# Layers 0 and 2 of a four-layer network: the rows of maxima alone are turned, and added to the queries by VectorE

## The chip, the core and the metric

The kernel runs on one core of a Trainium2 chip. A core has a matrix engine (TensorE, PE in the profile, with its weight loads as PEld), a vector engine (VectorE, DVE), a scalar engine (ScalarE, ACT), a general engine (GpSimd, POOL) and a queue engine that issues DMAs (SyncE, SP). Each runs a list of instructions of its own; semaphores make one wait for another. Work memory is SBUF, 128 partitions wide; the matrix engine writes to PSUM, which here is handed out in banks of 512 float32 columns. The metric is the device time of one execution in microseconds (us), and of several executions the median.

## The reference

The input `x` (16 batches, 256 tokens, 256 features) goes through four layers, each an attention part and a feed-forward part, every one behind a layer norm and with a residual sum. The change touches two attentions: the first part of layer 0, and the one inside layer 2's feed-forward part. Both have 16 heads of 16 features.

```python
# layer 0: queries are the normed x, memory is ctx (keys: first 256 features, values: last 256)
Q = _split_heads(query, 16) * 16 ** (-0.5)
logits = einsum('bhqd,bhkd->bhqk', Q, Kh) + b
logits = logits + MASK_VALUE * (1.0 - valid)[:, None, None, :]
weights = softmax(logits, axis=-1)
out = einsum('bhqk,bhkd->bhqd', weights, Vh)

# layer 2, inside its feed-forward part: causal self-attention
h = _rms(x, n1_w)
q = _rms(heads(wq), qn_w); k = _rms(heads(wk), kn_w); v = heads(wv)
scores = einsum('bhqd,bhkd->bhqk', q, k) * 16 ** (-0.5)
scores = where(causal, scores, -inf)
ao = einsum('bhqk,bhkd->bhqd', softmax(scores), v) @ wo.T
```

A softmax subtracts each row's maximum before the exponential. How that subtraction is made is what the change is about.

## The kernel before, in words

A batch's 256 tokens are two halves of 128 (`t` is 0 or 1). In each half, `qpad` holds 128 tokens (partitions) by 16 heads by 32 slots: 16 features and 16 slots for extras. `heads_transposed` (L277 to L282) turns it into the form that the scores need: four transposes on TensorE (L281) of four heads each (4 x 32 = 128 rows) into one bank of the pool `ptr`, then one copy by ScalarE (`evac`, L150 or L152) into SBUF. The result is `QT`: rows are slots, with four heads `j` in four bands of 32 rows, and four groups `c` along the columns. Head `4c + j` sits in band `j`, group `c`. The keys `KT` have the same form (`kpad` in layer 0, filled by DMA from the transposed context).

Scores are made twice. `score_max` (L223) makes them with the query tokens as rows, in four banks of the pool `pmm`; VectorE reduces each bank to its negated row maxima (`put` in `maxima`, L635 and L1492). The reductions write into a free slot of `qpad` (slot 17 in layer 0, 16 in layer 2). Then `queries` (layer 0) or `heads_q` (layer 2) turns the whole `qpad` once more, now with the maxima, into `QM`. `probs` (L241) makes the scores a second time, with the keys as rows, from `QM` and `KT`; the key rows of that slot are 1, so the product has the maximum already subtracted, and ScalarE takes the exponential (L263). `weighted` (L272) multiplies by the values, `back` turns the result to tokens again (L653) and divides.

In layer 0 rows 17 to 31 of each band of the keys are all 1 (the whole tile is set to 1, then the 16 features and the bias row 16 are loaded over it), and slots 18 to 31 of the queries are 0. In layer 2 slot 16 of each head's key is 1 and the other extras are 0.

The four compute engines run under a hand-written order (`manual_schedule`): what the Python code calls first stands first in each engine's list. Two lists, one for even and one for odd steps, are walked through; each entry names a piece of work and by how many steps its batch is away. Entries of layer 0's even list that the change and the prediction bear on:

```python
(maxima, -2, 3), (queries, -2, 0, QMs), (t_stats, 0), (exps, -1, 2), (queries, -3, 0, QTs),
(maxima, -2, 2), (slots, 1), (t_norm, 0), (values, -1, 1), (exps, -1, 3), (values, -1, 2),
(queries, -3, 1, QTs), (maxima, -3, 0), (v_heads, -2), (queries, -2, 1, QMs), (values, -1, 3),
(scatter, 4, 4), (exps, -2, 0), (back, -1, 1), (maxima, -3, 1), (turned, 0), (values, -2, 0),
```

In the odd list of layer 0, `(exps, -1, 3), (queries, -2, 1, QMs), (slots, 1), (maxima, -3, 0), (values, -1, 3), (queries, -3, 1, QTs)` come in this order. In layer 2's even list, the first making of `QM` stands behind `(maxima, 1, 2)` and is followed on `ptr` by `turned` of the cross-attention (L336); in its odd list the second stands behind `values` of the cross-attention (L358, with VectorE's L366 and L367) and is followed on `ptr` by `places` (L1592). Layer 2 mixes these with the products of the experts (L1676, L1703).

Pools: `ptr` has one bank in both layers; `pmm` has six in layer 0 and four in layer 2. In layer 0 the tile `o` (three buffers) takes the divided result of `back`; GpSimd adds it to `x` (L656). At the end of layer 0 the key and value projections of layer 3 begin, with loads into buffers that layer 0 no longer uses (`kv_load`, L476).

Of the kernel before, what the change touches and what calls it, by code (L numbers as in the profile page):

```python
# [9 lines left out]
F32 = mybir.dt.float32  # L10
# [28 lines left out]
def tile_kernel(ctx: ExitStack, tc: tile.TileContext, a, out):  # L39
# [237 lines left out]
    def heads_transposed(dst, src, h0, on=None, scale=None):  # L277
# [4 lines left out]
        evac(dst, p, scale, on=on)  # L282

    def normalized(t, O, dst):
        rec = small(16, "rec16")
        V.reciprocal(rec, O[:, :, 16])
        V.tensor_tensor(dst, O[:, :, :16], rec.unsqueeze(2).to_broadcast([P, 16, 16]), ALU.mult)
# [156 lines left out]
    with ExitStack() as l01:  # L444
# [87 lines left out]
        with ExitStack() as l0:  # L532
# [5 lines left out]

            bk = c0.tile([B, S], F32, name="bk")
            dma(bk, a["L0_b"].unsqueeze(0).to_broadcast([B, S]))  # L540
# [16 lines left out]
            for i in range(4):  # L557
# [3 lines left out]
                qpads.append(q)  # L561

            kpads, vpads = [], []
            for i in range(3):
                k = c0.tile([P, 4, S], F32, name=f"kpad{i}")
                V.memset(k, 1.0)
                kpads.append(k)
                v = c0.tile([P, 2, 16, 32], F32, name=f"vpad{i}")
                G.memset(v, 1.0)
                vpads.append(v)  # L570
# [47 lines left out]
            def q_norm(b):  # L618
                mv, r = mvs.pop(b)
                qps[b] = qpads[2 * (b % 2) : 2 * (b % 2) + 2]  # L620
                for t in range(2):
                    normed(qps[b][t][:, :, :16], b, t, mv, r, split=16)
                    G.memset(qps[b][t][:, :, 17], 0.0)
                QTs[b] = at[0].tile([P, 4, S], F32, name="QT", tag="QT")
                QMs[b] = at[0].tile([P, 4, S], F32, name="QM", tag="QM")
                oTs[b] = at[0].tile([P, 4, S], F32, name="oT", tag="oT")

            def queries(b, t, to):
                heads_transposed(to[b][:, :, t * P : (t + 1) * P], qps[b][t], 0, A)

            def maxima(b, u):
                t, cp = u // 2, u % 2

                def put(j, sc):
                    V.tensor_reduce(qps[b][t][:, 8 * cp + j : 8 * cp + j + 5 : 4, 17], sc, AX.X, ALU.max, negate=True)  # L635

                score_max(cp, t, QTs[b], KTs[b], 32, put)
# [133 lines left out]
            for b, tag in zip(range(KV0), ("QM", "QM", "oT", "oT")):  # L771
                kv_load(b, big4(tag), at[0].tile([P, S], F32, name="mrb0", tag="mrb0"))
            for b in range(KV0):
# [499 lines left out]
    with ExitStack() as l2:  # L1273
# [14 lines left out]
        with ExitStack() as l2a:  # L1288
# [44 lines left out]
            for i in range(2):  # L1333
                q = ta([P, 16, 32], f"qpad2{i}")
                V.memset(q, 0.0)
                qpads.append(q)
                k = ta([P, 16, 32], f"kpad2{i}")
                V.memset(k, 0.0)
                V.memset(k[:, :, 16], 1.0)
                kpads.append(k)  # L1340
                v = ta([P, 2, 16, 32], f"vpad2{i}")
                G.memset(v, 1.0)
                vpads.append(v)
# [108 lines left out]
            def head_scale(b):  # L1452
# [3 lines left out]
                for t in range(2):  # L1456
                    for k, to in ((0, qpads[t]), (1, kpads[t])):
# [3 lines left out]
                        )  # L1461
                    G.memset(qpads[t][:, :, 16], 0.0)
                del rqs[b]

            def heads_q(b, t, to):
                heads_transposed(to[b][:, :, t * P : (t + 1) * P], qpads[t], 0, A, hw[:, 0:1])

# [19 lines left out]
            def maxima(b, u):  # L1487
                t, cp = u // 2, u % 2
                qp = qpads[t]

                def put(j, sc):
                    V.tensor_reduce(qp[:, 8 * cp + j : 8 * cp + j + 5 : 4, 16], sc, AX.X, ALU.max, negate=True)  # L1492

                score_max(cp, t, QTs[b], KTs[b], 32, put, mask, True)
# [632 lines left out]
```

## Time and profile before

| what | value |
|---|---|
| median of 10 runs (lowest to highest) | 3187.6 us (3185.09 to 3191.82) |
| the profiled execution, its own time | 3187.92 us |
| its span, from the first instruction to the last | 3186.1 us |
| mean granted clock of TensorE | 0.939 |
| layer 0's attention | about 20 to 400 us |
| layer 2's attentions and first experts | about 1680 to 2660 us |
| transposes of `qpad` (L281), both layers | 512, of 272 ns (median) each |
| ScalarE's copies into `QM` | 32 of 586 ns (layer 0), 32 of 687 ns (layer 2) |
| VectorE's reductions into `qpad` | 256 of 683 ns (layer 0); 256, median 552 ns (layer 2) |
| GpSimd's memsets of the maxima slot | 64, of 122 ns (layer 0) and 132 ns (layer 2) |

The page gives each engine's busy time and share of the span. A row of the timeline gives start, length, engine, line, operation, what it writes and reads, shapes and count; in brackets stand the idle time before it on its engine and what ended that. Rows of one line that follow each other closely are merged, with one start and one length for all. A window's row gives the busy time of each engine in a stretch, how many instructions it had, and the granted clock of TensorE. A busy share is an average; an engine with a low share can still be the one that others wait for at one place, since each list runs in order.

### The profile page before, as it was taken

How to read it: one execution, taken by the hardware profiler on the slowest of the kernel's cores; microseconds unless marked ns; L12 is line 12 of the kernel's file. 1: busy time of each engine (PE TensorE's matmuls, PEld its weight loads, DVE VectorE, ACT ScalarE, POOL GpSimd, SP SyncE). 2: the span in 40 equal slices, each digit the busy share in tenths (PEclk: the TensorE clock that was granted, in tenths of full speed). 3: DMA queues.
4: the chain of work that ended last, by engine and by line, in shares of the span. 5: the costliest groups of instructions: out<-in, count | busy, mean ns of one | idle time of the engine just before them, and what ended most of it. 6: DMA issues, size and time to landing. Idle time of an engine off the chain costs nothing. (4 is left out here: it accounts for less than half of the span.)

```text
span 3186.1 us, 57308 instructions
## 1 busy us (share of the span) xinstructions
PE 2833.7 (89%) x22567; PEld 2026.7 (64%) x22567; DVE 1478.4 (46%) x3848; ACT 1159.4 (36%) x2192; POOL 911.9 (29%) x1459
## 2 busy tenths in 40 slices
PE   7999889999989992999967889999999999759995
PEld 4655466666668851688854446777777777636663
DVE  7766621100146640222224666666666651047776
ACT  3654421121112210111112435656656664224443
POOL 2445530000046516010011333233333221044543
PEclk9999999999999986999976989999999999869996
DMA  6941232122035322466640012333333236242211
GB/s 256 347 155 48 69 103 86 60 79 80 23 125 190 124 96 103 127 202 200 191 149 29 28 51 87 106 105 116 106 100 115 93 96 216 76 135 58 62 36 53
DMA packets 249375, 357.07 MB, mean 112 GB/s; under 512 B 24107, under 2 KB 189019, under 8 KB 244868
## 3 DMA queue, kind: packets, MB, share of 16 engines
q1 hardware_dynamic: 230660, 305.75, 29.3%
q0 software_dynamic: 18432, 47.47, 4.6%
q8 instruction: 187, 3.06, 0.4%
q14 instruction: 96, 0.79, 0.1%
HBM read 236.40 MB, written 117.52 MB: 111 GB/s over the span
## 5 line engine op out<-in xcount | busy, mean ns | idle before, releaser
L263 ACT ACTIVATE big<-pmm 128x512 f32<-128x512 f32 (+1 forms) x512 | 237.4, 550 | 118.8 <-PE pmm L256 103.8
L909 PE MATMUL pmm<-xiT,w 128*128 128x512 f32 x512 | 224.6, 596 | 2.1 <-DVE xiT L145 2.0
L157 POOL TENSOR_SCALAR rsq<-mv 128x2 f32<-128x2 f32 x128 | 26.7, 209 | 695.5 <-DVE mv L175 677.1
L917 PE MATMUL pacc<-w,h 128*128 128x256 f32 x1024 | 223.6, 379 | 0.0
L917 PEld LDWEIGHTS pacc<-w,h 128*128 128x128 f32 x1024 | 194.6, 190 | 33.3 <-issue 7.7
L918 DVE COPY yo<-pacc 128x256 f32<-128x256 f32 x64 | 27.2, 425 | 403.6 <-PE pacc L917 403.6
L945 POOL DMA_INDIRECT y<-ye,idx x64 | 62.0, 968 | 481.6 <-issue 481.2
L635 DVE TENSOR_REDUCE qpad<-pmm 128x2 f32<-128x512 f32 x256 | 158.9, 685 | 60.4 <-PE pmm L234 57.7
L316 DVE TENSOR_REDUCE max<-pmm 128x2 f32<-128x512 f32 x256 | 159.2, 681 | 31.4 <-PE pmm L234 28.4
L909 PEld LDWEIGHTS pmm<-xiT,w 128*128 128x128 f32 x512 | 96.0, 191 | 120.4 <-issue 111.0
L1492 DVE TENSOR_REDUCE qpad<-pmm 128x2 f32<-128x256 f32 (+1 forms) x256 | 125.1, 552 | 75.2 <-PE pmm L234 55.0
L1676 PE MATMUL pf<-hf,fw 128*128 128x256 f32 x640 | 152.5, 381 | 0.0
L1376 POOL DMA_INDIRECT y<-yslots,idx x64 | 66.0, 1031 | 289.3 <-SPq L1259 273.1
L1676 PE MATMUL pf<-xf,fw 128*128 128x256 f32 x576 | 142.7, 384 | 0.1
L911 ACT ACTIVATE h<-pmm 128x512 f32<-128x512 f32 x128 | 76.3, 597 | 149.7 <-PE pmm L909 149.6
L1676 PEld LDWEIGHTS pf<-hf,fw 128*128 128x128 f32 x640 | 116.8, 190 | 15.6 <-issue 2.0
L272 PE MATMUL pacc<-big,vpad 128*32 128x256 f32 (+1 forms) x2048 | 124.0, 366 | 1.0 <-ACT big L263 0.7
L234 PE MATMUL pmm<-kpad,QT 32*128 32x256 f32 x1024 | 107.9, 427 | 9.0 <-ACT big L263 7.5
L1676 PEld LDWEIGHTS pf<-xf,fw 128*128 128x128 f32 x576 | 103.2, 190 | 18.6 <-issue 6.7
L281 PE MATMUL ptr<-ident,qpad 128*128 128x128 f32 x512 | 85.4, 291 | 24.0 <-DVE qpad L184 12.1
L174 DVE BATCH_NORM_STATS2 bnst<-x 128x6 f32<-128x256 f32 x256 | 104.4, 408 | 4.8 <-POOL x L656 2.0
L1237 PE MATMUL pacc<-wd,hb 128*128 128x256 f32 (+1 forms) x432 | 99.2, 379 | 0.0
(462 smaller groups left out, 6114.8 us busy)
## 6 DMA issues: line engine op xcount, KB each, us to landing
xe<-zero SPq DMA_DIRECT2D x24, 1024.0 KB
w<-in_w_dram SPq DMA_DIRECT2D x16, 1024.0 KB
wg<-in_w_gate_dram SPq DMA_DIRECT2D x36, 352.0 KB
wu<-in_w_up_dram SPq DMA_DIRECT2D x36, 352.0 KB
xslots<-zero SPq DMA_DIRECT2D x9, 1024.0 KB
wd<-in_w_down_dram SPq DMA_DIRECT2D x36, 256.0 KB
xi<-xslots SPq DMA_DIRECT2D x36, 256.0 KB
yslots<-yb SPq DMA_DIRECT2D x36, 256.0 KB
```

The costliest lines, as they stand in the source:

```text
L174: V.bn_stats(st, xs[b][:, t, :])
L234: T.matmul(sc[j][:, i, :nk], lhsT=QT[rows, c, t * P : (t + 1) * P], rhs=KT[rows, c, :nk], start=(mask is None), stop=True, skip_group_chec ...
L263: A.activation(e[:, :, q0:], sc[j], AF.Exp, bias=bias, scale=scale)
L272: T.matmul(O[32 * j : 32 * j + 32, i, q0:], lhsT=lhsT(kc, 8 * cp + 4 * i + j), rhs=pT[j][:, i, q0:], start=(kc == 0 and i == 0), stop=(kc ...
L281: T.transpose(p[:, c, :], src[:, h0 + 4 * c : h0 + 4 * c + 4, :].rearrange("p h d -> p (h d)"), ident)
L316: V.tensor_reduce(self.m[:, t, j, :], sc, AX.X, ALU.max, negate=True)
L635: V.tensor_reduce(qps[b][t][:, 8 * cp + j : 8 * cp + j + 5 : 4, 17], sc, AX.X, ALU.max, negate=True)
L909: T.matmul(p, lhsT=w1[:, c, f * P : (f + 1) * P], rhs=xiT[:, c, :], start=(c == 0), stop=(c == 1))
L917: T.matmul(p[:, :D], lhsT=hT[f][:, s * P : (s + 1) * P], rhs=w2[:, f, :], start=(f == 0), stop=(f == 7))
L1237: T.matmul(p[:, t, :], lhsT=h[:m, k, t * P : (t + 1) * P], rhs=wd[:m, k, :], start=(k == 0), stop=(k == 2))
L1492: V.tensor_reduce(qp[:, 8 * cp + j : 8 * cp + j + 5 : 4, 16], sc, AX.X, ALU.max, negate=True)
L1676: T.matmul(p[:, j * S : (j + 1) * S], lhsT=w[:, c, f * P : (f + 1) * P], rhs=x, start=(c == 0), stop=(c == len(src) - 1),)
```

## The change

The maxima get tiles of their own, `mx` (128 tokens by 4 bands by 32 slots, zero elsewhere), two per batch parity and half. The reductions write there: for band `j` and group `c` into slot `17 + c` (layer 0) or `16 + c` (layer 2). Making `QM` is now one transpose of `mx` and one addition by VectorE: for each of the four groups, `QT` plus the turned maxima. All four groups of a band so carry the maxima rows of all four groups, and the keys pick the right one: group `c` of the keys has a 1 in row `17 + c` (or `16 + c`) and 0 in the other three. In layer 0 the keys are filled from `own`, a small pattern that GpSimd makes; in layer 2 four memsets set it. The memset of the maxima slot on GpSimd and ScalarE's copy into `QM` are gone. `bk` and layer 0's mask rows for the key projections now use buffers of `o`.

```diff
--- before.py
+++ after.py
@@ -281,6 +281,19 @@
             T.transpose(p[:, c, :], src[:, h0 + 4 * c : h0 + 4 * c + 4, :].rearrange("p h d -> p (h d)"), ident)
         evac(dst, p, scale, on=on)
 
+    def maxima_rows(pool):
+
+        rows = [[pool.tile([P, 4, 32], F32, name=f"mx{k}{t}", tag=f"mx{k}{t}") for t in range(2)] for k in range(2)]
+        for m in rows[0] + rows[1]:
+            V.memset(m, 0.0)
+        return rows
+
+    def less_maxima(QM, QT, t, mx):
+
+        p, tok = ptr()[:, :P], slice(t * P, (t + 1) * P)
+        T.transpose(p, mx.rearrange("p j c -> p (j c)"), ident)
+        V.tensor_tensor(QM[:, :, tok], QT[:, :, tok], p.unsqueeze(1).to_broadcast([P, 4, P]), ALU.add)
+
     def normalized(t, O, dst):
         rec = small(16, "rec16")
         V.reciprocal(rec, O[:, :, 16])
@@ -536,7 +549,7 @@
             psums(l0, "ps0", 6, 1, 1)
             l0.enter_context(tc.manual_schedule(engines=BUSY))
 
-            bk = c0.tile([B, S], F32, name="bk")
+            bk = at[0].tile([P, D], F32, name="o", tag="o", bufs=3)[:B]
             dma(bk, a["L0_b"].unsqueeze(0).to_broadcast([B, S]))
             lens_i = c0.tile([B, 1], I32, name="lens_i")
             dma(lens_i, a["itok"])
@@ -560,10 +573,17 @@
                 V.memset(q[:, :, 16], 1.0)
                 qpads.append(q)
 
+            own = c0.tile([P, 4], F32, name="own")
+            V.memset(own, 0.0)
+            for j in range(4):
+                rows = own[32 * j : 32 * j + 32]
+                G.affine_select(rows, rows, [[-1, 4]], ALU.not_equal, 1.0, base=-17, channel_multiplier=1)
+            mx0 = maxima_rows(c0)
+
             kpads, vpads = [], []
             for i in range(3):
                 k = c0.tile([P, 4, S], F32, name=f"kpad{i}")
-                V.memset(k, 1.0)
+                V.tensor_copy(k, own.unsqueeze(2).to_broadcast([P, 4, S]))
                 kpads.append(k)
                 v = c0.tile([P, 2, 16, 32], F32, name=f"vpad{i}")
                 G.memset(v, 1.0)
@@ -620,19 +640,21 @@
                 qps[b] = qpads[2 * (b % 2) : 2 * (b % 2) + 2]
                 for t in range(2):
                     normed(qps[b][t][:, :, :16], b, t, mv, r, split=16)
-                    G.memset(qps[b][t][:, :, 17], 0.0)
                 QTs[b] = at[0].tile([P, 4, S], F32, name="QT", tag="QT")
                 QMs[b] = at[0].tile([P, 4, S], F32, name="QM", tag="QM")
                 oTs[b] = at[0].tile([P, 4, S], F32, name="oT", tag="oT")
 
             def queries(b, t, to):
-                heads_transposed(to[b][:, :, t * P : (t + 1) * P], qps[b][t], 0, A)
+                if to is QMs:
+                    less_maxima(QMs[b], QTs[b], t, mx0[b % 2][t])
+                else:
+                    heads_transposed(to[b][:, :, t * P : (t + 1) * P], qps[b][t], 0, A)
 
             def maxima(b, u):
                 t, cp = u // 2, u % 2
 
                 def put(j, sc):
-                    V.tensor_reduce(qps[b][t][:, 8 * cp + j : 8 * cp + j + 5 : 4, 17], sc, AX.X, ALU.max, negate=True)
+                    V.tensor_reduce(mx0[b % 2][t][:, j, 17 + 2 * cp : 19 + 2 * cp], sc, AX.X, ALU.max, negate=True)
 
                 score_max(cp, t, QTs[b], KTs[b], 32, put)
 
@@ -769,7 +791,7 @@
 
             wsrc = kv_weights([big4("QT") for _ in range(2)])
             for b, tag in zip(range(KV0), ("QM", "QM", "oT", "oT")):
-                kv_load(b, big4(tag), at[0].tile([P, S], F32, name="mrb0", tag="mrb0"))
+                kv_load(b, big4(tag), at[0].tile([P, D], F32, name="o", tag="o", bufs=3))
             for b in range(KV0):
                 for i in range(4):
                     kv_piece(b, i, wsrc, pmm, ring[0])
@@ -1336,7 +1358,8 @@
                 qpads.append(q)
                 k = ta([P, 16, 32], f"kpad2{i}")
                 V.memset(k, 0.0)
-                V.memset(k[:, :, 16], 1.0)
+                for c in range(4):
+                    V.memset(k[:, 4 * c : 4 * c + 4, 16 + c], 1.0)
                 kpads.append(k)
                 v = ta([P, 2, 16, 32], f"vpad2{i}")
                 G.memset(v, 1.0)
@@ -1459,11 +1482,15 @@
                             to[:, :, :16], qks[b, t][:, 16 * k : 16 * k + 16, :],
                             rqs[b][1][:, t, 16 * k : 16 * k + 16].unsqueeze(2).to_broadcast([P, 16, 16]), ALU.mult,
                         )
-                    G.memset(qpads[t][:, :, 16], 0.0)
                 del rqs[b]
 
+            mx2 = maxima_rows(ca)
+
             def heads_q(b, t, to):
-                heads_transposed(to[b][:, :, t * P : (t + 1) * P], qpads[t], 0, A, hw[:, 0:1])
+                if to is QMs:
+                    less_maxima(QMs[b], QTs[b], t, mx2[b % 2][t])
+                else:
+                    heads_transposed(to[b][:, :, t * P : (t + 1) * P], qpads[t], 0, A, hw[:, 0:1])
 
             def heads_k(b, t):
                 heads_transposed(KTs[b][:, :, t * P : (t + 1) * P], kpads[t], 0, A, hw[:, 1:2])
@@ -1486,10 +1513,10 @@
 
             def maxima(b, u):
                 t, cp = u // 2, u % 2
-                qp = qpads[t]
+                mx = mx2[b % 2][t]
 
                 def put(j, sc):
-                    V.tensor_reduce(qp[:, 8 * cp + j : 8 * cp + j + 5 : 4, 16], sc, AX.X, ALU.max, negate=True)
+                    V.tensor_reduce(mx[:, j, 16 + 2 * cp : 18 + 2 * cp], sc, AX.X, ALU.max, negate=True)
 
                 score_max(cp, t, QTs[b], KTs[b], 32, put, mask, True)
```

## The prediction

> **What bounds the kernel now.** I read the page first, then the busy time of each engine over stretches of layers 0 and 2, then the timeline at places where the turned queries with maxima (QM) are made. Durations and instants are of the one profiled execution: its span is 3186.1 us and its own time 3187.92 us, 0.3 us from the median of 3187.6, so the sum can be set against either.
>
> ```profile
> PE 2833.7 (89%) x22567; PEld 2026.7 (64%) x22567; DVE 1478.4 (46%) x3848; ACT 1159.4 (36%) x2192; POOL 911.9 (29%) x1459
> ```
>
> ```profile
> 30.00:200.00 170.00, 164.32 (x1858) 105.75 (x1856) 126.78 (x286) 97.87 (x186) 65.85 (x105) 1.00 0.82 309
> 1940.00:2620.00 680.00, 672.45 (x7693) 501.63 (x7692) 418.12 (x1194) 418.17 (x778) 214.08 (x376) 1.00 0.33 104
> ```
>
> The columns after the length are PE, PEld, DVE, ACT and POOL busy, then the granted clock. In the steady part of both layers PE is busy 97% and 99% of the time: no other engine's average sets the end. But DVE is at 75% in layer 0, and all engines run an order fixed by hand, so what counts is how far DVE stands behind PE at each QM. An even step of layer 0, first QM (token half 0), then the second:
>
> ```profile
> 62.75 0.66 PE L281 MATMUL ptr<-ident,qpad 128*128 128x128 f32 x4
> 62.84 2.49 DVE L635 TENSOR_REDUCE qpad<-pmm 128x2 f32<-128x512 f32 x4 [0.29 <-PE pmm L234]
> 63.33 1.97 PE L256 MATMUL pmm<-QM,kpad 32*128 32x256 f32 x16
> 64.18 0.72 PEld L256 LDWEIGHTS pmm<-QM,kpad 32*128 32x128 f32 x10 [0.30 <-DVE qpad L635]
> 65.24 0.66 PE L281 MATMUL ptr<-ident,qpad 128*128 128x128 f32 x4
> ```
>
> ```profile
> 72.06 0.66 PE L281 MATMUL ptr<-ident,qpad 128*128 128x128 f32 x4
> 72.21 2.49 DVE L635 TENSOR_REDUCE qpad<-pmm 128x2 f32<-128x512 f32 x4 [2.74 <-PE pmm L234]
> 72.64 1.07 PE L272 MATMUL pacc<-big,vpad 128*32 128x256 f32 x16
> 72.75 0.59 ACT L150 COPY QM<-ptr 128x512 f32<-128x512 f32 x1 [0.79 <-PE ptr L281]
> 73.64 1.15 PE L256 MATMUL pmm<-QM,kpad 32*128 32x256 f32 x16
> ```
>
> The reader is to see that at both places DVE is in the middle of four reductions of the *next* maxima (2.49 us) while ACT, which had been idle, empties the transposes at once, and PE goes on.
>
> **The change, part by part.** *Removed from PE:* each of 64 QM makings (2 layers, 16 batches, 2 halves) has 1 transpose instead of 4. The row says 0.66 us for four, but the next matmul starts 0.58 us after the first (62.75 to 63.33), so a transpose takes 0.145 us of PE's time, three take 0.435 us, and 64 times that is 27.8 us. This is the ceiling of the gain. The built order shows the transposes at the same places with the rest of PE's list unchanged, so the change does what it says.
>
> *Where the 0.435 us is kept.* At 91.70 (odd step of layer 0):
>
> ```profile
> 91.70 0.66 PE L281 MATMUL ptr<-ident,qpad 128*128 128x128 f32 x4
> 91.85 2.06 ACT L263 ACTIVATE big<-pmm 128x512 f32<-128x512 f32 x4 [0.53 <-PE pmm L256]
> 92.29 1.82 PE L234 MATMUL pmm<-kpad,QT 32*128 32x256 f32 x16
> 92.99 0.72 PEld L234 LDWEIGHTS pmm<-kpad,QT 32*128 32x128 f32 x10 [0.20 <-ACT big L263]
> ```
>
> The 16 scores after it take 1.82 us instead of the 1.15 us that sixteen take at 73.64, because their banks come free only with ACT's exponentials. PE arriving 0.435 us earlier would wait 0.435 us longer there. So I count the odd steps of layer 0 at nothing (bounds: 15 calls by -0.435 = -6.5 us, and 0). If the exponentials did not cover it, PE would gain that time. In layer 2 I count the saving at nothing as well, where the next scores wait for ACT or DVE (bound -0.435 for some 10 calls, -4.4 us).
>
> *Removed from ACT:* 32 copies of 0.586 us and 32 of 0.687 us; ACT idles just before most of them. *Removed from POOL:* 64 memsets of 0.12 to 0.13 us that nothing in the steady part waits for. Both at nothing: what hides them is PE, and a loss is excluded, since nothing is put in their place there.
>
> *Added to DVE:* 64 additions of 512 columns with one operand in PSUM. The nearest rows are the 128x512 tensor-tensor instructions at L510 and L1228, 0.691 and 0.687 us: I take 0.69 (the 128x512 tensor-tensor at L1404 takes the same), 44 us in all, on an engine that is not full. The price is in the queue: the addition is built directly behind the reductions that stand before it in the hand-written order, and PE's next use waits for it. The ptr pool has one bank.
>
> Layer 0, even step, first QM: the reductions end at 65.33, the addition at 66.02, and with 0.1 us to PE the next user of ptr (transposes of the new queries, 65.24 in the row) starts at 66.12: 0.88 us late. That PE saves 0.435 us in front doesn't help: the middle of its scores waits for the same reductions (64.18 row). Second QM: the reductions end at 74.70, the addition 75.39, PE's exponent scores, which read this QM, start at 75.49 instead of 73.64: 1.85 us late. Behind them stand the back transposes, ACT's exponentials and the next maxima, all shifted with PE. The same pair of rows comes back in seven even steps from 62 to 345 us: 7 x 2.73 = 19.1 us. In odd steps the addition ends before PE's next user, but for one step with routing work on DVE (0.2 us late at 135.5 us).
>
> Layer 2, even and odd step:
>
> ```profile
> 2257.91 2.49 DVE L1492 TENSOR_REDUCE qpad<-pmm 128x2 f32<-128x512 f32 x4 [1.02 <-PE pmm L234]
> 2260.04 0.28 PE L336 MATMUL ptr<-ident_bf,nmp 128*128 128x128 bf16 x2
> ```
>
> ```profile
> 2211.73 1.76 DVE L366 RECIPROCAL rT<-pacc 128x256 f32<-128x256 f32 x1 [0.79 <-PE pacc L358]
> 2213.43 0.29 PE L1592 MATMUL ptr<-ohx,before 128*128 128x16 f32 x2
> 2213.52 0.42 DVE L367 TENSOR_TENSOR uT<-pacc,rT 128x256 f32<-128x256 f32 x1
> ```
>
> Even: reductions to 2260.40, addition and hand-over to 2261.19, while L336 needs the bank at 2260.04: 1.15 us, five times. Odd: the values' reciprocal and product stand ahead, to 2213.94; with the addition 2214.73, against L1592 at 2213.43: 1.30 us, six times; the first QM of odd steps adds 0.2 us five times (2202.60 against 2202.40). Together 5.8 + 7.8 + 1.0 = 14.6 us.
>
> *Ramps.* The same reading of the first calls gives 2.5 and 1.7 us of lateness in layer 0 (at 30 and 36 us) and 8.7 us over the first seven late calls of layer 2 (1740 to 1911), where PE has idle time to give: bounds 0 and 12.9, I take 3 + 5, and 1 for the last call of layer 2.
>
> *Start.* POOL's four small selects for `own` wait for a DVE memset that stands behind qpad's memsets (13.65 us). The nearest row is L84, 24 selects in 5.90 us: 4 x 0.25 = 1.0. The first key copy so starts at 14.9 instead of 13.80; three copies of 1024 columns at about 1.1 (the 256-column copy of L1128, 0.293, times four, as an upper bound; the memset's 0.91 as a lower) end 0.5 later still: +1.7 us (bounds 1.1 and 2.0), before PE has work.
>
> *Moved DMAs.* On SP, three mask rows for the key projections now use buffers of `o`, stand behind the contexts' loads and wait until POOL has read the last `o` (its last sum runs from 383.70 to 384.42). The next on SP, g_init, goes out at 404.49, and the first projection starts at 402.31: nothing is late, with 18 us of cover; without it the projection's first DVE step (L497) would wait for the row. Layer 2's four new memsets (0.17 us each by L128) run beside layer 1's products, at nothing.
>
> *Clock.* The new waits open gaps of about 2.2 us on PE (75.49 less 73.28, the end of L272 at 73.71 brought forward by 0.435) seven times. In the trace:
>
> ```profile
> 200.66:204.07 3.41, 1.07 (x6) 0.50 (x6) 0.26 (x1) 0.68 (x2) 1.55 (x2) 1.00 0.45 149
> 204.07:207.49 3.42, 3.18 (x15) 2.41 (x16) 1.84 (x4) 1.66 (x4) 1.27 (x2) 0.50 0.11 31
> ```
>
> A stretch with a PE gap of 2.26 us is followed by half clock (0.50); half clock for 3.41 us costs 1.7 us of PE's work. A gap of 0.84 us (270 us) was followed by one too, one of 1.54 us (2350) not. So between none and 18 (seven of 3.4 us in layer 0, eleven of 1.7 us in layer 2 would be 42 us): I take 8 us, four stretches of two windows in layer 0's seven, less what is gated by other engines.
> The Trainium skill ("TensorE: Matmul & The Clock Gate", section "What's actually happening") has the half clock come after an idle window of about 3.4 us. The rows show it after shorter gaps, and the row decides; by the rule these gaps would cost nothing and the sum would be 8 us less.
>
> *Sum.* 19.1 + 14.6 + 9 + 1.7 + 8 = 52.4; less 2 for three pauses (202, 251 and 299 us), in which ACT and DVE stand until one moment and PE would have waited anyway: +50. 3187.9 + 50 = 3238 us.
>
> **Rivals.** *Faster: DVE is in time.* DVE's reductions would have to be over about 0.8 us before PE's next user of the bank, so that the whole 27.8 us comes off PE: 3187.9 - 27.8 + 1.7 = 3162 us. For it: DVE is busy only 46%. Against it: at the even steps it ends after PE's next start even without the addition. 0.08.
> *Partly hidden.* One layer's waits are taken up by waits that exist, or the savings I put at nothing come: half of 33.7, some 9 for ramps and start, no clock, less up to 6: 3194 to 3215 us. For it: the order has slack at many ACT waits. 0.18.
> *The clock decides.* Most of the 18 gaps pull the half clock: the 44.4 without it plus 30 to 42: 3262 to 3275 us and a little beyond. For it: the 0.84 us gap; against: the 1.54 us gap. 0.15.
> *No change.* Gains and waits cancel: 0.04.
>
> **How the numbers follow.** The forecast, slower with waits as counted, has 0.55 and its own range is 3215 to 3262. Predicted 3238. The range for 8 in 10 takes most of the partly hidden case and the clock's: 3201 to 3278. About 0.2% is what a measurement can tell from no change: faster 0.08, same 0.04, slower 0.88.
>
> **What would show it.** After: in even steps of layer 0 PE idles about 2 us before the exponent scores, released by DVE's QM; in layer 2 waits of L336 and L1592 on DVE QM; additions of 0.69 us; 64 transposes for QM; PE's busy time falls though the span grows; more stretches at clock 0.50. Wrong would be additions that end before PE asks, or no new idle with QM as its releaser.

## The result, and the profile after the change

The changed kernel takes 3238.65 us (median of 8 runs, 3232.78 to 3244.66), the kernel before, run beside it, 3188.66 us (28 runs). The ratio is 1.0157 with an interval of 1.0145 to 1.0169: 50 us slower. The profiled execution of the changed kernel has a span of 3242.9 us and an own time of 3244.55 us.

The first part of its page, the busy time of each engine:

```profile
PE 2860.8 (88%) x22375; PEld 2034.7 (63%) x22375; DVE 1513.8 (47%) x3927; ACT 1122.2 (35%) x2128; POOL 910.2 (28%) x1399
```

TensorE has 192 instructions fewer (64 x 3), as the diff says, but its busy time is 27 us longer, not shorter. Two stretches tell why. They are the windows that answer to those shown of before, the second moved by 30 us because layer 2 begins some 26 us later (length, then PE, PEld, DVE, ACT, POOL busy, then the granted clock):

```profile
30.00:200.00 170.00, 153.05 (x1572) 95.21 (x1570) 121.42 (x273) 77.55 (x147) 56.09 (x78) 0.92 0.80 304
1970.00:2650.00 680.00, 658.69 (x7383) 484.75 (x7382) 423.17 (x1212) 398.37 (x742) 210.48 (x349) 0.99 0.32 102
```

In layer 0 TensorE's share fell from 97% to 90% and its clock from 1.00 to 0.92; in the steady part of layer 2 from 99% to 97%. It idles more, and part of what it does runs at half clock, which lengthens the busy time. (The five batches that fill up layer 2 last longer too, so the second window starts some 13 us earlier in the work than that of before; by the stages below, cut at the same work, the shares are again 99% and 97%.)

The places of the prediction, in the timeline of the changed kernel (start, length, engine, line; in brackets the idle time in front and what ended it). First an even step of layer 0, then an odd step of layer 2:

```profile
73.69 2.49 DVE L657 TENSOR_REDUCE mx<-pmm 128x2 f32<-128x512 f32 x4 [0.41 <-PE pmm L234]
...
76.09 0.68 DVE L295 TENSOR_TENSOR QM<-QT,ptr 128x512 f32<-128x512 f32 x1
76.83 1.11 PE L281 MATMUL ptr<-ident,qpad 128*128 128x128 f32 x4 [0.66 <-DVE QM L295]
...
85.13 2.48 DVE L657 TENSOR_REDUCE mx<-pmm 128x2 f32<-128x512 f32 x4 [2.67 <-PE pmm L234]
...
87.53 0.68 DVE L295 TENSOR_TENSOR QM<-QT,ptr 128x512 f32<-128x512 f32 x1
88.27 1.15 PE L256 MATMUL pmm<-QM,kpad 32*128 32x256 f32 x16 [1.89 <-DVE QM L295]
...
2257.18 1.76 DVE L379 RECIPROCAL rT<-pacc 128x256 f32<-128x256 f32 x1 [1.05 <-PE pacc L371]
2258.97 0.42 DVE L380 TENSOR_TENSOR uT<-pacc,rT 128x256 f32<-128x256 f32 x1
2259.32 0.68 DVE L295 TENSOR_TENSOR QM<-QT,ptr 128x512 f32<-128x512 f32 x1
2260.05 0.39 PE L1619 MATMUL ptr<-ohx,before 128*128 128x16 f32 x2 [1.00 <-DVE QM L295]
```

The addition starts the moment DVE's work in front of it is over, takes 0.68 us, and TensorE's next user of the bank (L281, L1619) or of the sum (L256) starts right behind it. Each of these starts is later than TensorE was free: by 0.66, 1.89 and 1.00 us.

The waits of TensorE for such a sum, from the view of waits of the changed kernel (engine, tile and line that waited, what it waited for, us in all, times, longest; `...` stands for waits of another kind). Layer 0, from 62 us to its end, then its first batches (20 to 62 us):

```profile
PE pmm L256 <- DVE QM L295: 7.9, 4, 2.1
...
PE pmm L256 <- issue: 5.9, 3, 2.2
...
PE ptr L281 <- DVE QM L295: 4.6, 7, 0.7
...
PE ptr L281 <- DVE QM L295: 3.3, 1, 3.3
PE pmm L256 <- DVE QM L295: 2.6, 1, 2.6
```

Layer 2, from 2050 us to its end, then its first batches (1700 to 2050 us); L349 and L1619 are L336 and L1592 of before:

```profile
PE ptr L349 <- DVE QM L295: 5.8, 5, 1.2
PE ptr L1619 <- DVE QM L295: 5.7, 5, 2.0
...
PE pmm L256 <- DVE QM L295: 1.1, 1, 1.1
PE ptr L201 <- DVE QM L295: 1.0, 4, 0.3
...
PE ptr L349 <- DVE QM L295: 5.8, 2, 2.9
...
PE ptr L1619 <- DVE QM L295: 3.6, 2, 2.6
...
PE pmm L256 <- DVE QM L295: 2.4, 1, 2.4
...
PE ptr L201 <- DVE QM L295: 0.5, 2, 0.3
```

Four of the seven waits of L256 in layer 0 are named after the addition; three of the same length have "issue" as releaser. They are the same wait (13.8 us in seven): each of the three ends right behind an addition, as here.

```profile
221.94 0.68 DVE L295 TENSOR_TENSOR QM<-QT,ptr 128x512 f32<-128x512 f32 x1
...
222.68 1.36 PE L256 MATMUL pmm<-QM,kpad 32*128 32x256 f32 x16 [1.89 <-issue]
```

### The profile page after: what moved, and what is told of

It reads as the page before. It is cut to its first block, busy times and chain, and to the rows that moved or that the text cites. A ratio compares the mean times of both kernels' runs of the same rounds, so it can differ in the third digit from the quotient of the medians.

```text
span 3242.9 us, 56857 instructions
## 1 busy us (share of the span) xinstructions
PE 2860.8 (88%) x22375; PEld 2034.7 (63%) x22375; DVE 1513.8 (47%) x3927; ACT 1122.2 (35%) x2128; POOL 910.2 (28%) x1399
## 5 line engine op out<-in xcount | busy, mean ns | idle before, releaser
L657 DVE TENSOR_REDUCE mx<-pmm 128x2 f32<-128x512 f32 x256 | 158.8, 684 | 51.5 <-PE pmm L234 51.5
L1519 DVE TENSOR_REDUCE mx<-pmm 128x2 f32<-128x256 f32 (+1 forms) x256 | 125.0, 550 | 67.2 <-PE pmm L234 61.1
L256 PE MATMUL pmm<-QM,kpad 32*128 32x256 f32 x1024 | 93.6, 419 | 16.5 <-DVE QM L295 10.5
L1730 PE MATMUL pf<-fw,hf 128*128 128x192 f32 x512 | 98.7, 337 | 4.0 <-DVE hf L1721 2.6
```

The source lines that it names most:

```text
L256: T.matmul(sc[j][:, i, :], lhsT=KT[rows, c, kc * P : (kc + 1) * P], rhs=QT[rows, c, q0:], start=(minus is None and mask is None), stop=Tru ...
L657: V.tensor_reduce(mx0[b % 2][t][:, j, 17 + 2 * cp : 19 + 2 * cp], sc, AX.X, ALU.max, negate=True)
L1519: V.tensor_reduce(mx[:, j, 16 + 2 * cp : 18 + 2 * cp], sc, AX.X, ALU.max, negate=True)
L1730: T.matmul(p[:, t * S : t * S + D - M], lhsT=hs[b // 2, src][f // 2][:, f % 2, t * P : (t + 1) * P], rhs=w[:, f, :], start=(f == 0), stop= ...
```

## The experiments

None of them ran on the chip of the first measurement: e1 to e8 ran on a second chip, e9 and e10 on a third, e11 on a fourth. On these three the kernel before takes 3066 to 3071 us, with a mean clock of 0.950 to 0.951, so ratios to it are compared, and stages. A stage is cut at TensorE's back transposes: layer 0 from 20 us to the first back transpose of its last batch, the ramp of layer 2, in which its line of batches fills up, from 85 us ahead of its first back transpose to that of its fifth batch, the steady part from there to that of its last. All results first:

```
run                        median us  before    ratio   interval
e1 only layer 0             3102.13   3066.04   1.0116  1.0096-1.0136
e2 only layer 2             3099.64   3066.04   1.0112  1.0091-1.0133
e3 four turns               3119.58   3066.04   1.0172  1.0155-1.0189
e4 before, copy on DVE      3123.61   3066.04   1.0184  1.0166-1.0202
e5 the change again         3141.93   3070.47   1.0227  1.0210-1.0245
e6 turned earlier           3093.96   3070.47   1.0075  1.0058-1.0091
e7 bank freed by ACT        3114.96   3070.47   1.0142  1.0120-1.0164
e8 sum on POOL              3082.79   3070.47   1.0040  1.0024-1.0056
e9 three edits              3073.91   3068.62   1.0015  0.9999-1.0032
e10 e9, four turns          3073.65   3068.62   1.0016  1.0002-1.0030
e11 e9, four turns in ramp  3067.27   3067.90   1.0002  0.9991-1.0012
```

And by stage, worked out from the traces: length / idle time of TensorE / time at half clock, in us. The first two rows are the kernels before and after on the first chip. "As before" is layer 0 of e2 and layer 2 of e1, which no edit touched, on the second chip. Each row is one profiled execution, which can be some us off the median of its runs (e6's is 8 us faster, e9's 4 us slower).

```
             layer 0               ramp of layer 2        steady part of layer 2
1st, before  358.8 / 21.9 / 20.5   318.0 / 44.8 /  75.1   638.8 /  6.2 / 0.0
1st, change  379.8 / 38.6 / 47.8   335.5 / 52.0 / 120.3   650.1 / 19.8 / 3.4
as before    337.2 /  8.7 /  6.8   312.2 / 42.1 /  61.4   630.2 /  0.3 / 0.0
e5 change    374.0 / 33.7 / 44.4   333.7 / 49.1 / 123.7   641.6 / 14.0 / 3.4
e3           366.0 / 30.2 / 23.9   324.6 / 46.4 /  96.5   641.3 / 10.4 / 0.0
e4           361.6 / 31.2 / 13.7   322.7 / 47.3 /  86.5   643.0 / 11.5 / 0.0
e6           347.4 / 19.7 / 13.7   324.3 / 47.3 /  99.0   634.5 /  8.9 / 0.0
e7           368.0 / 25.1 / 27.3   327.2 / 42.9 / 120.4   630.3 /  5.2 / 0.0
e8           350.0 / 16.1 / 23.9   320.8 / 46.8 /  85.3   627.0 /  2.2 / 0.0
e9           338.3 /  8.9 /  0.0   323.5 / 42.3 / 105.8   627.0 /  2.1 / 0.0
e10          341.9 /  8.9 /  0.0   312.3 / 42.6 /  58.0   629.4 /  0.3 / 0.0
e11          339.6 /  9.3 /  0.0   311.9 / 41.8 /  61.4   627.3 /  1.9 / 0.0
```

**e1 and e2: one layer at a time.** The hunks of the other layer are taken back; one line of each is shown.

```diff
 # e1: layer 2 as before
-            mx2 = maxima_rows(ca)
 # e2: layer 0 as before
-            mx0 = maxima_rows(c0)
```

> The change in layer 0 alone, layer 2 as in the kernel before. By the prediction's own terms layer 0 costs 19.1 us of waits in even steps, 3 of ramp, 1.7 of start and 8 of clock, 32 us in all: about 3220 us. By the trace of the changed kernel, in which the back transposes of the last batch of layer 0 came 21 us later than before: about 3210 us. Rival: layer 0 alone loses little and layer 2 makes the loss (under 3195 us).

> The change in layer 2 alone, layer 0 as before. By the prediction's terms 14.6 us of waits and 6 of ramps: about 3208 us. By the trace of the changed kernel, whose back transposes in layer 2 fell behind by another 34 us: about 3222 us, most of it in the first five batches. If the two layers' losses add, this run's and the other's sum to the 50 us of the whole change, within 6 us.

Measured: +36.1 and +33.6 us. Layer 0 lost more than both figures expected (32 and 22); layer 2 lost more than by the prediction's terms (20.6) and as much as the trace of the changed kernel had let expect (34). Their sum, 69.7, is not 50.

**e5: the change again, on this chip.** No edit.

> The changed kernel itself, unaltered, on the chip of this group of runs, so that the others have it beside them. On the chip of the first single-layer runs the kernel before took 3066 us where it took 3188 us on the chip of the prediction, and layer 0 as before lasted 298 us there instead of 323 us (first to last back transposes). If the loss is one of waits in the hand-written order, the ratio is again 1.014 to 1.023; if it came with the slower chip, it is under 1.008.

Measured: +71.5 us, so the two layers do add up (69.7), and the loss does not come with the slower chip; it is larger on the faster one. The stages say the same: 36.8 in layer 0, 21.5 in the ramp, 11.4 in the steady part. Why layer 0 lost only some 21 us on the first chip (its last batch came that much later) is read from the windows of before there, and of layer 0 as before (e2) here:

```profile
240.00:300.00 60.00, 54.07 (x573) 33.66 (x572) 37.22 (x88) 29.00 (x55) 32.43 (x44) 0.91 0.17 53
```

```profile
240.00:300.00 60.00, 59.28 (x677) 38.47 (x676) 44.68 (x101) 34.49 (x67) 38.35 (x54) 1.00 0.20 64
```

On the first chip the kernel before already had TensorE pauses, two of them among those named in the prediction, and a clock of 0.91 in this stretch; on the second it had neither. The changed kernel has the same waits for the sums on both chips, 50.2 us (with the three under "issue") and 50.1 us, and the same time at half clock in the three stages, 171.5 us. It is the kernel before that differs: in layer 0 TensorE's idle time grew by 16.7 us on the first chip (21.9 to 38.6) and by 25.0 on the second (8.7 to 33.7), so on the first the new waits in part took the place of pauses. What makes the pauses, and why one chip has them, was not found out.

**e4: the kernel before, with its copies of the turned queries on DVE.** Nothing else of the change is in it. The line of layer 0 is shown; that of layer 2 has the same edit.

```diff
-                heads_transposed(to[b][:, :, t * P : (t + 1) * P], qps[b][t], 0, A)
+                heads_transposed(to[b][:, :, t * P : (t + 1) * P], qps[b][t], 0, V if to is QMs else A)
```

> The kernel before, with one edit: the copies that empty the four transposes of the queries with maxima are made by DVE in place of ACT, 64 of them. No key row, no maxima rows, no addition, no moved load. Theory (the loss is the place in DVE's queue, behind the reductions that stand ahead in the hand-written order): most of the loss comes, 3215 to 3240 us. Rival (DVE's queue is harmless, and the loss comes from the addition's length, the key copies, the moved loads or the start): 3185 to 3200 us.

Measured: +57.6 us, above the expected range, on the side of the theory. The waits of its TensorE and the rows of its copy, in layer 0 and in layer 2, where it multiplies by a weight as well:

```profile
PE pmm L256 <- DVE QM L145: 14.5, 9, 2.3
...
PE ptr L336 <- DVE QM L147: 9.7, 7, 2.6
PE ptr L1592 <- DVE QM L147: 8.8, 7, 2.4
PE ptr L281 <- DVE QM L145: 8.7, 11, 2.9
```

```profile
L145 DVE COPY QM<-ptr x32: 657/681/694, 32.5 to 368.3; 128x512 f32<-128x512 f32 x32
...
L147 DVE TENSOR_SCALAR QM<-ptr,hw x32: 736/743/750, 1667.5 to 2575.2; 128x512 f32<-128x512 f32 x32
```

The same four waits at the same lines, and the copy takes 0.68 us in layer 0, as the addition does, and 0.74 in layer 2 (least, median, longest in ns). So no key row, maxima row, moved load or addition as such is needed for the loss: the place in DVE's queue is enough. It is not all of the 71.5 us; e4 keeps its four transposes, and its ratio, 1.0184, is that of the changed kernel with four transposes (1.0172, e3 below).

**e6: the additions earlier in DVE's queue.** Only the hand-written order is altered; the entries that moved are shown, with those beside them.

```diff
-                (maxima, -2, 3), (queries, -2, 0, QMs), (t_stats, 0), (exps, -1, 2), (queries, -3, 0, QTs),
+                (queries, -2, 0, QMs), (maxima, -2, 3), (t_stats, 0), (exps, -1, 2), (queries, -3, 0, QTs),
-                (queries, -3, 1, QTs), (maxima, -3, 0), (v_heads, -2), (queries, -2, 1, QMs), (values, -1, 3),
+                (queries, -2, 1, QMs), (maxima, -3, 0), (queries, -3, 1, QTs), (v_heads, -2), (values, -1, 3),
-                (maxima, 1, 2), (heads_q, 1, 0, QMs), (f_part, 5, 1, 7, 1),
+                (heads_q, 1, 0, QMs), (maxima, 1, 2), (f_part, 5, 1, 7, 1),
-                (f_part, 5, 0, 5, 1), (f_end, 5, 0, 5), (x_step, 0, "values", 0), (heads_q, 1, 1, QMs),
+                (f_part, 5, 0, 5, 1), (heads_q, 1, 1, QMs), (f_end, 5, 0, 5), (x_step, 0, "values", 0),
```

> The changed kernel with only the hand-written order altered: each addition stands ahead of the reductions, or of the values' reciprocal and product, that it stood behind. Layer 0 even step: first QM ahead of the fourth group of maxima, second QM ahead of the next batch's first maxima. Layer 2: even first QM ahead of the third maxima, odd second QM ahead of the values of the cross attention. Theory (the loss is the wait in DVE's queue): the four waits of the prediction's sum (19.1 and 14.6 us) and most of the ramps go, ratio to before 0.992 to 1.003; if the transposes' time is then collected too, towards 0.992. Rival (addition, key copies, clock or loads cost by themselves, wherever the addition stands): ratio 1.010 or more, as the changed kernel.

Measured: 1.0075, so 0.0152 of the 0.0227 are gone, two thirds of the loss; the theory had nearly the whole (0.992 to 1.003). All waits for the sums that are left in the whole execution, and two that are new:

```profile
PE ptr L281 <- DVE QM L295: 3.9, 3, 1.3
...
PE ptr L201 <- DVE QM L295: 1.7, 6, 0.4
PE pmm L256 <- DVE QM L295: 1.7, 2, 1.1
```

```profile
PE ptr L294 <- ACT xf L152: 5.9, 6, 1.0
...
PE ptr L294 <- DVE mx L657: 5.4, 2, 3.1
```

The waits for the sums fell from 50.1 us (e5) to 7.3; but where the transposes of the maxima (L294) now come too early, TensorE waits in front of them instead: 5.4 us for the reductions, at two places in layer 0, and 5.9 us, six times in layer 2, for ACT to empty the bank. By the stages 10.2 us are left in layer 0, 12.1 in the ramp of layer 2, with half clock for 99 us, and 4.3 in its steady part.

**e7: ACT frees the bank, DVE adds later.** It splits the waits for the bank from those for the sum.

```diff
-        V.tensor_tensor(QM[:, :, tok], QT[:, :, tok], p.unsqueeze(1).to_broadcast([P, 4, P]), ALU.add)
+        m = at[0].tile([P, P], F32, name="mt", tag="mt", bufs=1)
+        A.copy(m, p)
+        V.tensor_tensor(QM[:, :, tok], QT[:, :, tok], m.unsqueeze(1).to_broadcast([P, 4, P]), ALU.add)
```

> The changed kernel, but ACT copies the one turned maxima tile (128x128) out of the bank, and DVE adds it from that copy at the same place of its queue. What waits for the bank (L281 in layer 0, L349 and L1619 in layer 2) is let go by ACT at once; what waits for the sum itself (the exponent scores) still waits for DVE. By the prediction's terms the bank waits are 7 x 0.88 + 5.8 + 7.8 = 19.8 us and the waits for the sum 7 x 1.85 + 1 = 14 us. Theory of the two kinds of wait: a third to a half of the loss goes, ratio 1.007 to 1.012. Rival (one kind only): nothing goes (1.015 or more), or nearly all (under 1.005).

```profile
PE pmm L256 <- DVE QM L297: 24.9, 18, 2.6
...
PE ptr L351 <- ACT mt L296: 0.7, 2, 0.4
...
PE ptr L1621 <- ACT mt L296: 0.4, 1, 0.4
PE ptr L281 <- ACT mt L296: 0.4, 1, 0.4
```

The waits at L281, L349 and L1619 (L351 and L1621 in this kernel) are gone but for 1.5 us, and 37% of the loss with them (1.0142 against 1.0227), a share as expected; the ratio itself lies above the range given, which was made before the 1.0227 was known. The waits of the exponent scores at L256 grew instead, from 20.3 us in e5 to 24.9: TensorE, less often stopped by the bank, meets the late sum.

**e8: the sum on POOL.** As e7, with the last line on POOL.

```diff
-        V.tensor_tensor(QM[:, :, tok], QT[:, :, tok], m.unsqueeze(1).to_broadcast([P, 4, P]), ALU.add)
+        G.tensor_tensor(QM[:, :, tok], QT[:, :, tok], m.unsqueeze(1).to_broadcast([P, 4, P]), ALU.add)
```

> As the one before, and POOL makes the addition from ACT's copy, so that DVE has no part in QM at all and its queue can't delay it. POOL's 256-column additions of layer 0 take 0.72 us, so an estimate for 512 columns is 1.4 us, on an engine that is busy 28%. Theory (DVE's queue is the loss): bank waits go, and the sum is late by about 1 us at the second even QM of layer 0 only: ratio 1.000 to 1.008. Rival (a sum on any engine but ACT's direct copy is as late): 1.013 or more.

```profile
L297 POOL TENSOR_TENSOR QM<-QT,mt x64: 1254/1265/1302, 32.9 to 2542.0; 128x512 f32<-128x512 f32 x64
```

```profile
PE pmm L256 <- POOL QM L297: 9.0, 10, 1.8
```

Measured: 1.0040, as the theory had it. The addition takes 1.27 us here, nearly twice as long, on a queue that stood idle until ACT's copy ahead of 41 of the 64, and four fifths of the loss are gone. From e7 (1.0142) only the engine of the addition differs. What cost the time is not the length of the addition.

**e3: the three transposes put back into the changed kernel.** The same maxima rows are turned four times, and the addition reads all four; the lines that shape the bank for it are left out here.

```diff
-        T.transpose(p, mx.rearrange("p j c -> p (j c)"), ident)
+        for c in range(4):
+            T.transpose(p[:, c, :], mx.rearrange("p j c -> p (j c)"), ident)
```

> The changed kernel with the three transposes put back: the same four maxima rows are turned four times into the same bank (the result is the same; only the saving on TensorE is gone), 64 x 0.435 = 27.8 us of TensorE's work more than the changed kernel has. Theory (the saving was worth nothing, for TensorE waited for DVE, ACT or the bank behind it): 3235 to 3245 us, as the changed kernel. With the prediction's bounds for odd steps (6.5 and 4.4 us) at most 3250. Rival (the saving was collected in full): 3266 us.

Measured: 1.0172 against 1.0227 of e5: with 27.8 us of TensorE's work more it is about 17 us *faster*, and the intervals lie apart. No theory had that. The windows of both by stage, the change first:

```profile
20.00:394.00 374.00, 340.25 (x3537) 209.76 (x3537) 272.29 (x650) 176.97 (x337) 158.59 (x210) 0.94 0.46 171
1642.00:1976.00 334.00, 284.81 (x2952) 177.79 (x2952) 196.89 (x545) 131.94 (x269) 93.72 (x156) 0.81 0.15 48
```

```profile
20.00:386.00 366.00, 335.76 (x3633) 212.99 (x3633) 271.83 (x650) 176.76 (x337) 158.10 (x210) 0.97 0.47 175
1636.00:1960.00 324.00, 277.61 (x2978) 175.12 (x2978) 196.20 (x542) 131.74 (x269) 92.74 (x154) 0.85 0.15 49
```

With the extra transposes the granted clock is 0.97 instead of 0.94 in layer 0 and 0.85 instead of 0.81 in the ramp of layer 2, and TensorE is busy for *less* time with *more* matmuls. Over the three stages TensorE's idle time fell from 96.8 to 87.0 us, so part of the transposes lies where it had waited, and the time at half clock fell from 171.5 to 120.4 us. That the higher clock makes the gain is argued from these figures; e9 to e11 go on with it.

**e9 and e10: a version without the waits, and the transposes put back into that.** e9 is e8 with the second QM of layer 0's even steps moved as in e6, and with the start mended (POOL clears the key pattern, ACT makes the key copies).

```diff
-            V.memset(own, 0.0)
+            G.memset(own, 0.0)
-                V.tensor_copy(k, own.unsqueeze(2).to_broadcast([P, 4, S]))
+                A.copy(k, own.unsqueeze(2).to_broadcast([P, 4, S]))
```

> Three edits to the changed kernel together: ACT copies the turned maxima out of the bank and POOL adds (as in the run with the sum on POOL, which was 1.0040 of before); the second QM of layer 0's even steps stands ahead of the next batch's first maxima; at the start POOL clears the small key pattern and ACT, idle there, makes the three key copies. What was left in the run with the sum on POOL: 7.0 us of waits for the sum in layer 0, 1.7 us of later start, and half clock for 85 us in layer 2's ramp where layer 2 as before had 61. Theory: the first two go and the first transposes of queries start at about 17 us instead of 21.4, and some of the clock with them: ratio 0.994 to 1.001. Rival (PE's lists are bound elsewhere, the new slack is taken up by POOL's or DVE's other work): 1.002 to 1.006.

> As the one before, with the three transposes put back (turned four times, only the first result used): 64 x 0.435 = 27.8 us of TensorE's work more, in a kernel that has nearly no wait for QM. In the changed kernel the same edit made the whole faster (1.0172 against 1.0227). Theory (there the extra work lay inside waits and kept the clock up; here nothing hides it): slower than the one before by 10 to 28 us, 0.3 to 0.9%. Rival (the transposes lie in gaps in any case): within 0.2%, or faster.

e9 has no loss left in layer 0 (338.3 us; 337.2 as before) and gains 3.2 us in the steady part of layer 2. The first transposes of the queries start at 16.53 us (21.46 in the changed kernel, 19.67 in the one before), which is no longer to be seen at the end of layer 0. Its ratio, 1.0015, is just above the range of the theory, for in its profile the ramp of layer 2 takes 11 us more than before at nearly the same idle time. e10 has the same median: by the profiles it gives 3.6 and 2.4 us away in layer 0 and the steady part, 6.0 us for some 23.5 us of transposes there (54 of the 64 places, at 0.435 us), and gets 11 back in the ramp. The theory on e10 missed; the rival's range was met, but not for its reason: the sum is level, its parts are not. The 11 us are those of two executions. Over all twelve runs of each kernel the mean clock is 0.945 in e9 and 0.950 in e10, which is some 30 us less at half clock (the two profiles differ by 48 in the ramp), so the usual gain in the ramp is smaller, an estimate from the level medians being 6 us.

**e11: four turns in the ramp alone.**

```diff
-                    less_maxima(QMs[b], QTs[b], t, mx2[b % 2][t])
+                    less_maxima(QMs[b], QTs[b], t, mx2[b % 2][t], 4 if b < 6 else 1)
```

> As the kernel of the best three edits (e9), with the maxima turned four times only for batches 0 to 5 of layer 2, 36 extra transposes in all; once everywhere else. With four turns everywhere, layer 2's ramp had half clock for 58 us instead of 106 and lasted 312 us instead of 324, while layer 0 and the steady part of layer 2 took 3.6 and 2.4 us more. Theory (TensorE's extra work keeps its clock up in the ramp, and is worth little elsewhere): half clock in the ramp near 60 us, ramp near 312 us, layer 0 and the steady part as in e9 (338 and 627 us): ratio 0.996 to 0.9995, below both of its parents. Rival (the difference of the ramps came from one profiled execution, or from layer 0's end): ramp 320 us or more, ratio 1.0005 to 1.003.

Two windows of the ramp, first of e9, then of e11:

```profile
1690.00:1760.00 70.00, 57.31 (x671) 35.24 (x669) 40.34 (x118) 28.08 (x62) 24.89 (x36) 0.85 0.11 33
1760.00:1830.00 70.00, 58.62 (x603) 34.62 (x603) 45.47 (x132) 22.62 (x52) 29.42 (x44) 0.78 0.16 52
```

```profile
1690.00:1760.00 70.00, 56.40 (x728) 35.56 (x725) 43.97 (x126) 29.60 (x65) 26.52 (x39) 0.95 0.12 33
1760.00:1830.00 70.00, 57.88 (x703) 33.83 (x699) 48.41 (x138) 26.66 (x61) 31.99 (x46) 0.95 0.19 59
```

Every stage came as expected: ramp 311.9 us with 61.4 at half clock, layer 0 339.6, steady part 627.3. In the windows TensorE is busy about as long (58.62 and 57.88 us), but gets through 703 matmuls instead of 603, some of them the transposes put back, at a clock of 0.95 instead of 0.78. Over all runs the mean clock of the whole span is 0.942 to 0.949 in e9 and 0.947 to 0.953 in e11, so the higher clock isn't one execution; nor is it the other chip, for the kernel before has 0.951 on both. The whole, 1.0002 (0.9991 to 1.0012), is just above the range expected: level with the kernel before, not faster. From e9 it differs by 0.0013, within the intervals. No version of this study beats the kernel before.

## Why the prediction was right, and where its sum was not

Its mechanism is shown. e4 makes most of the loss with nothing but the place in DVE's queue; e6 and e8 take most of it away by another place or another queue, with the rest of the change left in. The rest, some 14 of e5's 71.5 us by e4 and 17 by e3, comes with the three transposes taken away, which the prediction had at nothing. Of the rivals, "DVE is in time" and "no change" fall with the waits above; "partly hidden" came true for layer 0 on the first chip alone, through its pauses (its own terms give 3208 at least, not 3194: 3187.9 + 16.9 + 9 - 6); "the clock decides" has too high a total, but the half clock did grow at a place that the forecast left out. The price of the addition holds (0.69 predicted, 0.68 measured). That of the start holds in its sum (+1.7 and +1.8) by luck: the key copies began at 14.25 us and not at 14.9, and the three took 4.44 us, more than the prediction's 1.1 each.

The sum, term by term, against the waits of the changed kernel's profile on the first chip:

```
term                         predicted   measured
layer 0, even steps            19.1      18.4   (4.6 + 7.9 + 5.9)
layer 2, steady                14.6      12.5   (5.8 + 5.7 + 1.0)
layer 2, last call              1         1.1
ramp of layer 0                 3         5.9   (3.3 + 2.6)
ramp of layer 2                 5        12.3   (5.8 + 3.6 + 2.4 + 0.5)
start                           1.7       1.8
```

The waits read from the rows of before hold within 0.7 us in layer 0 and 2.1 us in the steady part of layer 2. Even the number of them does: seven in layer 0, five at L349; L1619 had five, not six.

**The ramps were mis-sized.** The step that failed is "where PE has idle time to give: bounds 0 and 12.9, I take 3 + 5". The waits came to 18.2 us, above the upper bound. TensorE's idle time in the ramp of layer 2 grew by 7.2 us only (44.8 to 52.0) at 12.3 us of waits, so other idle time there did shrink; but the waits at QM were not shorter for it.

**The clock was counted in one place of two.** The prediction counted 8 us for the gaps of 2 us in layer 0 and nothing for the ramp of layer 2. In layer 0 the half clock grew by 27 us on the first chip and by 38 on the second, where it costs at most half of that, 14 and 19 us; in e5 seven of its eight stretches from 76 to 360 us begin within 1 us of the end of a wait for a sum, three behind the waits of some 2 us and four behind those of 0.66 us, which had been given no price. In the ramp the half clock grew from 75 to 120 us on the first chip and from 61 to 124 on the second, the largest change of clock in the kernel. Part of that comes without any wait: in e9 the waits at QM and its bank are down to 4 us and the idle time is as before, and half clock is 106 us in its profile, against 58 in that of e10 with the transposes back. And "PE's busy time falls" was wrong for the same reason.

**The savings were put at nothing, and were worth less.** They were counted at 0, with a gain of 6.5 and 4.4 us as bounds. In the changed kernel the missing transposes cost some 17 us (e5 against e3, second chip), beyond the bounds on the other side. Only once no wait hides the result are the three transposes worth something: 3.6 us in layer 0 and 2.4 in the steady part of layer 2, by the profiles of e10 and e9. Of the ceiling of 27.8 us these 6.0 are there, and the ramp takes as much or more back.

**That the total met the time owes something to cancelling.** Layer 0 was put at 32 us with its start and clock and lost some 21 on the first chip, where pauses took part of it; layer 2 was put at 20.6 and lost more: 17.5 us in the ramp (335.5 against 318.0) and 11.3 in the steady part (650.1 against 638.8). On the second chip, without the pauses, layer 0 lost 36.8 and the whole 71.5. The prediction's 50 is the value of a chip with pauses, not of the mechanism; that the terms put too low (ramps, clock, transposes) and the pauses that took some of the loss came out at 50 is luck.

## What to carry to other kernels

When work goes to another engine, price it at each call by what stands ahead of it in that engine's queue and by who needs the result or the bank next, not by its length: 1.27 us on POOL's queue, idle ahead of most of them, cost 0.0040 of the time in e8, 0.68 us behind DVE's reductions 0.0142 in e7. Work taken off the engine with the highest share is worth only what it does not wait for a moment later; putting it back, once the new waits are gone, measures that directly. Where TensorE waits often, taking work off it can go with a lower clock and cost more than the work was worth: compare the granted clock, and not the busy time alone.

## What the hardware showed that was not expected

Half clock came after windows in which TensorE was mostly busy. In the changed kernel on the second chip:

```profile
117.52:120.93 3.41, 2.75 (x23) 1.60 (x20) 3.36 (x6) 1.21 (x3) 0.00 (x0) 1.00 1.03 344
120.93:124.35 3.42, 3.42 (x28) 1.94 (x30) 1.39 (x6) 1.34 (x3) 2.34 (x4) 0.50 1.02 416
124.35:127.76 3.41, 3.41 (x52) 1.86 (x44) 1.82 (x4) 2.19 (x5) 2.94 (x4) 1.00 1.03 413
```

A single gap of 0.66 us, with TensorE at 2.75 of 3.41 us, and the next 3.42 us run at 0.50, after which the clock is back. It isn't so after each: in layer 0 of that run, from 76 to 360 us, four of the seven waits of 0.66 us and three of the seven of some 2 us are followed by such a stretch. In the ramp of layer 2 the state lasts: three stretches of 17.1 us at 0.50 in e9, after windows of 3.41 us with 1.0 to 1.1 us of idle time. With 36 transposes of 0.145 us more, 5.2 us of work, the half clock of the ramp is 61.4 us in the profile of e11, where e9's has 105.8. Which measure of activity the clock goes by, these runs don't settle. The Trainium skill ("TensorE: Matmul & The Clock Gate", section "What's actually happening") has the slow state after an idle window of about 3.4 us and the fast one after a busy window of that length. The length of the window agrees with these rows; that a window must be idle does not.
